# Batch 0's x turned by VectorE, the queries' weights loaded once, and three loads moved, in a cross-attention kernel on one core

## The chip, the cores and the metric

The kernel runs on one core of a Trainium2 chip. The time is the device time of one execution in microseconds (us), the median of several runs. A core has five engines, each with an instruction queue of its own: TensorE (PE in the profile; its weight loads are listed as PEld), VectorE (DVE), ScalarE (ACT), GpSimd (POOL) and SyncE (SP). SP does no arithmetic here; its queue issues most of the transfers (DMAs). ScalarE's queue issues a few too. Each issue holds its queue for about half a microsecond to one microsecond, and the data lands later.

## The reference

Attention of 8 batches of 112 queries over 375 context rows, of which the last 4 are "prompts" with a softmax of their own. There are 20 heads of 16 channels (320 channels); a context row has 512 elements. Everything is float32.

```python
text, ip = ehs[:, :-4], ehs[:, -4:]
q, k, v = heads(x @ W_q), heads(text @ W_k), heads(text @ W_v)
p = softmax(q @ k.T * 16 ** -0.5)
text_out = p @ v
k_ip, v_ip = heads(ip @ W_k_ip), heads(ip @ W_v_ip)
qsem = l2norm(p @ text)                  # 512 elements for each query and head
sem = qsem @ l2norm(ip).T
p_ip = softmax(q @ k_ip.T * 16 ** -0.5 + 0.5 * sem) * spatial_mask
out = (text_out + p_ip @ v_ip) @ W_out + b_out + x
```

## The kernel before

The work goes in steps (b, g): batch b, group g of four heads, five groups to a batch. A step n has the number 5b + g. In each step

- `multiplied` (L787 on) multiplies the transposed probabilities xgT by a table u, which holds the Gram matrix of the batch's context in blocks of 32 rows beside its values. The four results go to four banks ps_qd. From them come the length of qsem, its products with the prompts and the text's output, without qsem itself ever being formed;
- `scores` (L719) makes the scores of the step two ahead (`LEAD`), four of them, in the two banks ps_sc or, for one pair, the two banks ps_mm;
- `probabilities` (L754) takes the maximum nmx on VectorE (L751) and the exponential p on ScalarE (L765; for batches from 1 on with a copy ipl of the prompts' logits, L767). `sent` (L769, the issue at L772) sends p from SP to xg, which regroups queries by 32 rows, one transfer for a head;
- `turned` (L774) turns xg with VectorE's 32x32 transposes into xgT (L781) for the step after;
- `reduced` (L846) multiplies ps_qd by p and sums, on VectorE. With that, and with ScalarE's copy pvs (L813), the banks ps_qd are free for the next step.

Between the steps the engines make the next batch's tables: `values` (L611), `keys` (L577; its third block, heads 16 to 19, only transposes keys that `values` made on the side, L568), `gram` (L535), `project_queries` (L381). Batch 0 has its queries alone; batches 1 and 2, 3 and 4, and so on share a pass. For batch 0 x comes as rows, and TensorE turns it (L359, copied by ScalarE at L362); for the others x is loaded by `load_x_blocks` (four transfers, 28 rows by 4 by 80 elements, into xr_sb, which has two places), and VectorE turns it in 32x32 blocks (L369). The rows of the weights W_q must be in the matching order: `load_channels` gives the one for TensorE's way, `load_pairs` the one for VectorE's. So the queries' weights are loaded twice, at L133/L134 and again at L121/L122. `spread` (L143, L144) spaces the last four heads to 32 columns on GpSimd and is run after each.

The order of instructions on TensorE, VectorE and SP is the order in which the program is written. In the prologue, up to the first step, this holds for all engines. An engine takes its instructions in that order, and a wait at one holds up all behind it. In the prologue SP issues, in order: context of batch 0, the values' weights, x of batch 0, the queries' weights, the keys' weights, context of batch 1, twelve copies of ug into u (`gram_to_groups`, L553; four more go through ScalarE's queue), vr (values regrouped, L636, out of a copy vd that ScalarE sends at L627), xg of step 0, then the queries' weights again, x of batch 1, xg of step 1, the prompts' weights wkip and wvip (L137), and xg of step 2. At the end of step 0 follow the context of batch 2 (L160, L165) and x of batch 2 (`x_loads`, L127). `kip` (L328) holds the prompts' keys, `ps_ip` (L708) the prompts' logits of batch 0.

PSUM has eight banks in three rings: four ps_qd, two ps_sc, two ps_mm. `bank(name, spare)` (L85) takes the next of ps_mm, or with `spare` the next of ps_sc. A ring's next bank is free when the last reader of what was in it is done.

Of the kernel before, what the change touches and what calls it, by code (L numbers as in the profile page):

```python
# [8 lines left out]
F32 = mybir.dt.float32  # L9
# [11 lines left out]
def kernel(  # L21
# [14 lines left out]
    nc = tc.nc  # L36
    P = 128
    B, S, C = x.shape
# [46 lines left out]
    def bank(name, spare=False):  # L85

        if spare:
            return ps_sc.tile([P, 512], F32, tag="sc", name=name)
        return ps_mm.tile([P, 512], F32, tag="mm", name=name)
# [28 lines left out]
    def load_pairs(eng, t, w):  # L118

        w = w.rearrange("(p c) f -> p c f", c=5)  # L120
        eng.dma_start(t[0::2, :, :C], w[:, :3, :])  # L121
        eng.dma_start(t[1::2, :2, :C], w[:, 3:, :])  # L122

    def load_x_blocks(b, j):

        for a in range(QN):
            nc.sync.dma_start(  # L127
                xr_sb[a * RG : a * RG + S // QN, j, :, :XB],
                x[b, :, a * XB : (a + 1) * XB].rearrange("(q i) f -> i q f", q=QN),
            )  # L130

    def load_channels(eng, t, w):
        eng.dma_start(t[:, :FULL, :C], w[: FULL * P, :].rearrange("(i p) f -> p i f", p=P))  # L133
        eng.dma_start(t[:REST, FULL, :C], w[FULL * P :, :])  # L134

    def load_embed(eng, t, w):
        eng.dma_start(t[:, :, :C], w.rearrange("(p e) f -> p e f", e=NE))  # L137
# [48 lines left out]

    wv_in = work.tile([P, BLK, P], F32, tag="xgT", name="wv_in")
    wv_in = wv_in.rearrange("p j k -> p (j k)")[:, : NE * C].rearrange("p (e f) -> p e f", f=C)
    load_embed(nc.sync, wv_in, w_v)
    nc.sync.dma_start(x_sb[:, 0, :], x[0])  # L190
    load_channels(nc.sync, wq_sb, w_q)
    load_embed(nc.sync, wk_sb, w_k)
    loaded[1] = load_ctx(1)


    ident = const.tile([P, P], F32, tag="ident", name="ident")
    make_identity(nc, ident)
    nc.gpsimd.memset(wq_sb[REST:, FULL, :], 0.0)

    half = const.tile([P, NT, P], F32, tag="half", name="half")  # L200
    nc.gpsimd.memset(half, 1.0)
# [143 lines left out]
    def project_queries(bs):  # L345
        n = len(bs)
        end = bs[0] == B - 1
        xT = work.tile([P, NC, 2, QN, RG], F32, tag="xT", name=f"xT_{bs[0]}", bufs=1)
        qm = work.tile([P, NC, 2, 2 * S], F32, tag="qm", name=f"qm_{bs[0]}", bufs=2)

        qT = const.tile([P, NC, S], F32, tag="qT", name="qT") if bs[0] == 0 else None
        for j, b in enumerate(bs):
            queries[b] = (qT, qm, j)
        if qT is not None:
            nc.gpsimd.memset(xT[REST:, FULL, 0], 0.0)
            for i in range(NC):
                cn = min(P, C - i * P)
                ps = ps_qd.tile([P, 512], F32, tag="qd", name=f"ps_x_0_{i}")
                nc.tensor.transpose(  # L359
                    ps[:cn, :S], x_sb[:, 0, i * P : i * P + cn], ident[:S, :S]  # L360
                )
                nc.scalar.copy(  # L362
                    xT[:cn, i, 0, :, : S // QN],
                    ps[:cn, :S].rearrange("p (q i) -> p q i", q=QN),
                )
                yield
        for j in range(n if qT is None else 0):
            for e in range(NC):
                nc.vector.transpose(  # L369
                    xT[:, e, j],  # L370
                    xr_sb[:, j, :, e : e + XB]
                    .rearrange("p q (m c) -> p q m c", c=5)[:, :, :, 0:4:3],
                )
            yield
        for i in range(NC):
            if end and i == FULL:
                ps = ps_qd.tile([P, 512], F32, tag="qd", name=f"ps_q_{bs[0]}_{i}")
            else:
                ps = bank(f"ps_q_{bs[0]}_{i}")
            for j in range(NC):  # L380
                nc.tensor.matmul(  # L381
                    ps[:, : n * S],
                    wq_sb[:, j, i * P : (i + 1) * P],
                    xT[:, j, :n, :, : S // QN],
                    start=(j == 0),
                    stop=(j == NC - 1),
                )

            for r in range(2 if i < FULL else 1):
                nc.vector.tensor_scalar_mul(  # L390
                    qm[:, i, r, : n * S], ps[:, : n * S], emask[:, r : r + 1]
                )
            if qT is not None:
                nc.scalar.copy(qT[:, i, :], ps[:, :S])
            yield
# [162 lines left out]
    def keys(b):  # L558
        s = st[b]
        if b > 0:  # L560
            nc.gpsimd.tensor_copy(s["kT"][:, :, TT:], kip[:, :, b * NIP : (b + 1) * NIP])
        for i in range(NC):
            ps = bank(f"ps_k_{b}_{i}", spare=1 < b < B - 1 and i == FULL)
            if 0 < b < B - 1 and i == FULL:

                for c in range(NT):
                    rows = min(P, TT - c * P)
                    nc.tensor.transpose(  # L568
                        ps[:, c * P : c * P + rows],
                        s["k3"][:rows, c].rearrange("p a r d -> p (a r d)"),  # L570
                        ident[:rows, :rows],
                    )
                nc.scalar.copy(s["kT"][:, i, :TT], ps[:, :TT])
                yield
                return
            for e in range(NE):
                nc.tensor.matmul(  # L577
                    ps[:, :TT],
                    wk_sb[:, e, i * P : (i + 1) * P],
                    s["ctxT"][:, e, :TT],  # L580
                    start=(e == 0),
                    stop=(e == NE - 1),
                )
            nc.scalar.copy(s["kT"][:, i, :TT], ps[:, :TT])
            yield
# [545 lines left out]
    def run(key, make, pieces=1):  # L1131

        if key not in gens:
            gens[key] = make()
        for _ in range(pieces):
            next(gens[key], None)
# [63 lines left out]
    nc.scalar.preload_act_table(AF.Exp)  # L1200
    gram_to_groups(0, range(QN - 1))
    run(("v", 0), lambda: values(0))
    run(("q", 0), lambda: project_queries(pairs[0]), 3)
    gram_to_groups(0, (QN - 1,), nc.scalar)
    run(("v", 0), None, 2)
    values_to_dram(0, nc.scalar)
# [1 line left out]
    spread(nc.gpsimd, wq_sb)  # L1208
    nc.gpsimd.tensor_copy(wv_sb[:, :, C:], wk_sb[:, :, FULL * P : C])
    spread(nc.gpsimd, wk_sb)  # L1210
    nc.gpsimd.memset(xr_sb, 0.0)
    for xt in x_ring:
        nc.gpsimd.memset(xt, 0.0)
    run(("q", 0), None)
# [4 lines left out]
        probabilities(0, 0, a)  # L1219
    drain(transposed_context(1))  # L1220
    run(("q", 0), None)
    nc.gpsimd.memset(wq_sb[:, FULL, :], 0.0)
    load_pairs(nc.sync, wq_sb, w_q)
    load_x_blocks(1, 0)
    run(("k", 0), None)
    for a in range(GROUP):
        scores(0, 1, a, early=True)
        probabilities(0, 1, a)
    load_embed(nc.sync, wkip_sb, w_k_ip)
    load_embed(nc.sync, wvip_sb, w_v_ip)  # L1230
    placed(0, 0)
    drain(turned(0, 0, BLK))
    run(("k", 0), None)
    run(("v", 1), lambda: values(1))
    more_constants()
    spread(nc.gpsimd, wq_sb)
    prologue.close()

    def load_x(b0, b1):
# [2 lines left out]
    def load_rest(n):  # L1242
# [8 lines left out]


    x_loads = {
        (0, 0): ((0, 0), (2, 1)),
        (1, 0): ((3, 0), (4, 1)),
        (2, NG - 1): ((5, 0), (6, 1)),
        (4, NG - 1): ((7, 0),),
# [17 lines left out]
    for n, (b, g) in enumerate(steps[:-NG]):  # L1275
# [11 lines left out]
        for j, _ in enumerate(multiplied(b, g)):  # L1287
            if j == 0:
                for c, a in now if late else ():
                    scores(*c, a)  # L1290
                    probabilities(*c, a)
                if g == 3:
                    regrouped(b + 1, nc.gpsimd.tensor_copy, [(a, a) for a in range(GROUP)])
                    regrouped(b + 1, nc.scalar.copy, across[0])
                elif g == NG - 1:
                    regrouped(b + 1, nc.scalar.copy, across[2])
                for c, a in more:
                    scores(*c, a, ps=bank(f"ps_s_{c[0]}_{c[1]}_{a}"))
                    probabilities(*c, a, hold=True)
                if n == NG - 1:  # L1300
                    run(("c", LEAD), None)
            if j == 5:
                for c, a in then:
                    scores(*c, a)
                held = more + [(c, a) for c, a in then if c == steps[n + LEAD + 1]]
                for c, a in then:
                    probabilities(*c, a, hold=(c, a) in held)
                drain(turn)
                for c, a in held:
                    sent(*c, a)  # L1310
            if j == 2:
                if g == 0:
                    gram_banks(b + 1)
                turn = turned(*steps[n + 1], 2 * QN)
                next(turn)
                if 1 <= g <= 3:
                    gram_to_groups(b + 1, {1: (0,), 2: (1,), 3: (3,)}[g], parts=halves[g == 2])
                for c, i in x_loads.get((b, g), ())[: int(n > 0)]:
                    load_x_blocks(c, i)

                if g in (1, 2) and b > 0:
                    run(("f", b - 1), None)
# [43 lines left out]
    b = B - 1  # L1366
# [136 lines left out]
```

## Time and profile before

| | |
|---|---|
| median of 3 runs | 418.91 us (417.69 to 419.31) |
| the profiled execution's own time | 419.28 us |
| its span in the trace | 417.6 us |
| mean granted clock of TensorE | 0.999 |
| busy: TensorE, VectorE, ScalarE, GpSimd | 98%, 80%, 52%, 30% |
| steps 0, 1, 2, 3 start at | 37.06, 49.47, 58.83, 68.89 us |
| steps 4, 5, 6 start at | 79.32, 87.59, 97.95 us |

A row of the timeline gives the start, the busy time, the engine, the line and the operation with its output and inputs (`out<-in`), the tile as partitions by elements, and a count (xN) where rows were joined; the start is then that of the first and the time that of all. In brackets stands how long the engine was idle before it, and what released it. `SPq` and `ACTq` are the queues that issue transfers: their times are the times of issuing, not of the transfer. A row of the chain gives start, time and piece. The rows on which the argument rests are shown in the prediction.

### The profile page before, as it was taken

What the parts mean: (1) busy time and instruction counts of PE and PEld (TensorE: products, weight loads), DVE (VectorE), ACT (ScalarE), POOL (GpSimd) and SP (SyncE); (2) the same over time, 40 slices, a digit from 0 to 9 for tenths busy, and PEclk for the clock granted to TensorE, in tenths of its full rate; (3) what the DMA queues carried; (4) which work ended last, traced back from release to release, by engine and by line L of the source; (5) the groups of instructions that cost most, each with busy time, mean ns of one, the idle gap of its engine ahead of it and who ended that gap; (6) DMA issues with size and microseconds to landing.
All of it is one profiled execution on the core that took longest, in us unless ns stands there. A gap on an engine that the chain in (4) does not pass through costs nothing.

```text
span 417.6 us, 14139 instructions
## 1 busy us (share of the span) xinstructions
PE 410.9 (98%) x5505; PEld 322.8 (77%) x5505; DVE 333.9 (80%) x726; ACT 217.0 (52%) x730; POOL 123.3 (30%) x308
## 2 busy tenths in 40 slices
PE   8999999999999999999999999999999999999995
PEld 8866777878777877788778887788777987787893
DVE  4036688998798988899799988889888977889774
ACT  2344332746356363654538463553637553688773
POOL 3621121112052120712135120611207121555540
PEclk9999999999999999999999999999999999999999
DMA  8677946565954555545554455545544356444300
GB/s 252 187 192 198 187 111 163 143 169 132 195 152 118 151 149 146 140 125 153 143 142 127 127 154 142 145 106 153 163 119 115 92 167 162 130 129 127 111 2 31
DMA packets 47578, 58.98 MB, mean 141 GB/s; under 512 B 10648, under 2 KB 41536, under 8 KB 47510
## 3 DMA queue, kind: packets, MB, share of 16 engines
q1 hardware_dynamic: 46878, 57.10, 51.9%
q8 instruction: 44, 0.72, 0.8%
q10 hardware_dynamic: 632, 0.96, 0.8%
q14 instruction: 24, 0.20, 0.2%
HBM read 16.79 MB, written 1.88 MB: 45 GB/s over the span
## 4 chain that ended last, share of the span: by engine, by line
PE 90%; DMA 3%; DVE 2%; ACT 2%; issue 1%; SPq 1%; POOL 0%; DVEq 0%; ACTq 0%; POOLq 0%
PE ps_qd L800 38%; PE ps_v L611 15%; PE ps_s L729 10%; PE ps_k L577 10%; PE ps_g L535 7%; DMA xg<-p 3%; PE ps_o L1017 3%; PE ps_q L381 2%; PE ps_g L491 1%; PE ps_w L472 1%; DVE nmx L751 1%; PE ps_k L593 1%; PE ps_c L455 1%; ACT p L765 0%; DVE xgT L781 0%
## 5 line engine op out<-in xcount | busy, mean ns | idle before, releaser
L800 PE MATMUL ps_qd<-u,xgT 32*112 32x168 f32 (+11 forms) x3840 | 218.6, 350 | 0.0
L800 PEld LDWEIGHTS ps_qd<-u,xgT 32*112 32x112 f32 x3840 | 186.0, 172 | 26.1 <-DVE ss L846 1.3
L765 ACT ACTIVATE p<-ps_s,nmx 112x371 f32<-112x371 f32 x156 | 84.5, 579 | 91.2 <-DVE nmx L751 83.9
L781 DVE STREAM_TRANSPOSE xgT<-xg 128x512 f32<-128x512 f32 (+2 forms) x79 | 126.0, 1603 | 6.2 <-DMA xg<-p 4.6
L751 DVE TENSOR_REDUCE nmx<-ps_s 112x1 f32<-112x371 f32 x160 | 78.5, 535 | 26.2 <-PE ps_s L729 25.3
L846 DVE CUSTOM_DVE_ANT_0 junk<-ps_qd,p 112x371 f32<-112x371 f32 x146 | 79.3, 543 | 19.7 <-ACT pvs L813 4.0
L698 POOL COPY u<-vr 128x64 f32<-128x64 f32 x120 | 26.5, 239 | 137.3 <-PE ps_qd L800 104.9
L729 PE MATMUL ps_s<-kT,qm 32*112 32x375 f32 (+1 forms) x320 | 66.4, 496 | 0.0
L611 PE MATMUL ps_v<-wv_sb,ctxT 128*128 128x384 f32 (+1 forms) x192 | 63.0, 477 | 0.0
L611 PEld LDWEIGHTS ps_v<-wv_sb,ctxT 128*128 128x128 f32 x192 | 35.7, 190 | 20.9
L577 PE MATMUL ps_k<-ctxT,wk_sb 128*128 128x371 f32 x136 | 46.9, 488 | 0.2 <-DVE ctxT L463 0.2
L729 PEld LDWEIGHTS ps_s<-kT,qm 32*112 32x112 f32 x320 | 25.9, 171 | 12.3 <-issue 10.0
L577 PEld LDWEIGHTS ps_k<-ctxT,wk_sb 128*128 128x128 f32 x136 | 24.4, 189 | 14.1 <-issue 0.5
L646 ACT COPY vr<-vext 32x240 f32<-32x240 f32 x84 | 32.7, 389 | 1.2
L618 ACT COPY vext<-ps_v 128x384 f32<-128x384 f32 (+1 forms) x24 | 11.2, 466 | 41.0 <-PE ps_v L611 41.0
L535 PE MATMUL ps_g<-ctxT 128*32 128x375 f32 (+11 forms) x672 | 30.4, 333 | 0.0
L535 PEld LDWEIGHTS ps_g<-ctxT 128*32 128x32 f32 x672 | 27.7, 110 | 2.0
L767 ACT COPY ipl<-ps_s 112x4 f32<-112x4 f32 x140 | 23.1, 165 | 0.0
L992 POOL TENSOR_TENSOR wv<-vip,w 112x1280 f32<-112x1280 f32 x6 | 14.8, 2466 | 26.4 <-DVE w L929 26.4
L390 DVE TENSOR_SCALAR qm<-ps_q,emask 128x224 f32<-128x224 f32 (+1 forms) x25 | 9.0, 394 | 16.5 <-PE ps_q L381 16.5
L507 ACT ACTIVATE ug<-ps_g 128x375 f32<-128x375 f32 (+2 forms) x24 | 8.3, 375 | 24.6 <-PE ps_g L535 12.4
L442 DVE STREAM_TRANSPOSE ctxT<-ct 128x512 f32<-128x512 f32 x18 | 20.0, 1110 | 0.0
(174 smaller groups left out, 342.2 us busy)
## 6 DMA issues: line engine op xcount, KB each, us to landing
xg<-p SPq DMA_DIRECT2D x156, 162.3 KB
u<-ug SPq DMA_DIRECT2D x124, 99.0 KB
ct<-in_ctx_dram SPq DMA_DIRECT2D x24, 176.0 KB
vip<-vipd SPq DMA_DIRECT2D x6, 560.0 KB
out_dram<-ob SPq DMA_DIRECT2D x8, 140.0 KB
ct<-in_ctx_dram SPq DMA_DIRECT2D x4, 256.0 KB
x_sb<-in_x_dram SPq DMA_DIRECT2D x7, 140.0 KB
xr_sb<-in_x_dram SPq DMA_DIRECT2D x28, 35.0 KB
```

Source lines behind the costliest of these rows:

```text
L535: nc.tensor.matmul(ps[c][q * RG : (q + 1) * RG, j * RG - c * P : T - c * P], ctxT[:, e, j * RG : (j + 1) * RG], ctxT[:, e, j * RG : T], st ...
L577: nc.tensor.matmul(ps[:, :TT], wk_sb[:, e, i * P : (i + 1) * P], s["ctxT"][:, e, :TT], start=(e == 0), stop=(e == NE - 1),)
L611: nc.tensor.matmul(ps[:, :w], ctxT[:, e, c * P : (c + 1) * P], wv_sb[:, e, :w], start=(e == 0), stop=(e == NE - 1),)
L646: copy(s["vr"][a * RG : (a + 1) * RG, q::QN].rearrange("p c g d -> p c (g d)"), s["vext"][q * RG : (q + 1) * RG, :, a * w : (a + 1) * w],)
L698: nc.gpsimd.tensor_copy(v, dealt(b, c, s["vr"][:, c * QN : (c + 1) * QN, g, :]))
L729: nc.tensor.matmul(ps[:S, :w], qm[a * RG : (a + 1) * RG, i, r, j * S : (j + 1) * S], s["kT"][a * RG : (a + 1) * RG, i, :w], start=True, st ...
L751: nc.vector.tensor_reduce(nmx, s["sc", g, a][:S, :TT], AX.X, ALU.max, negate=True)
L765: nc.scalar.activation(s["p", g][:, a, :], ps[:S, :TT], AF.Exp, bias=nmx)
L767: nc.scalar.copy(s["ipl"][:, groups[g][a], :], ps[:S, TT:T])
L781: nc.vector.transpose(xT[:, j0:j1].rearrange("p j (k q) -> p q j k", q=QN), xg[:, :, j0 * RG : j1 * RG].rearrange("p q (j k) -> p q j k", ...
L800: nc.tensor.matmul(banks[a][:S, j * RG : UW], xT[a * RG : (a + 1) * RG, j, :S], region(b, c)[a * RG : (a + 1) * RG, q, j * RG - c * P :], ...
L846: nc.vector.tensor_tensor_reduce(out=junk, in0=ps[:S, :TT], in1=s["p", g][:, a, :], scale=1.0, scalar=0.0, op0=ALU.mult, op1=ALU.add, accu ...
```

## The change

- Batch 0's x is loaded by `load_x_blocks` into the second place of xr_sb, and VectorE turns it. TensorE's three transposes, ScalarE's three copies and a clearing of xT on GpSimd go. xr_sb is cleared first thing, since its loads now come early.
- The queries' weights are loaded once, by `load_pairs`, and spread once. Their third block is cleared ahead of that.
- x of batch 1 is loaded right behind the context of batch 1, ahead of the copies of u. x of batch 2 is loaded behind xg of step 0, where the second load of the weights and x of batch 1 stood, and wkip next to it, ahead of xg of step 1. wvip stays behind xg of step 1. At the end of step 0 no x is loaded any more.
- The third block of batch 1's keys takes a bank of ps_sc in place of one of ps_mm, as it does for later batches already.

```diff
+    ident = const.tile([P, P], F32, tag="ident", name="ident")
+    make_identity(nc, ident)
+    nc.gpsimd.memset(xr_sb, 0.0)
+    nc.gpsimd.memset(wq_sb[:, FULL, :], 0.0)
     load_embed(nc.sync, wv_in, w_v)
-    nc.sync.dma_start(x_sb[:, 0, :], x[0])
-    load_channels(nc.sync, wq_sb, w_q)
+    load_x_blocks(0, 1)
+    load_pairs(nc.sync, wq_sb, w_q)
     load_embed(nc.sync, wk_sb, w_k)
     loaded[1] = load_ctx(1)
-    ident = const.tile([P, P], F32, tag="ident", name="ident")
-    make_identity(nc, ident)
-    nc.gpsimd.memset(wq_sb[REST:, FULL, :], 0.0)
+    load_x_blocks(1, 0)
...
-        if qT is not None:
-            nc.gpsimd.memset(xT[REST:, FULL, 0], 0.0)
-            for i in range(NC):
-                cn = min(P, C - i * P)
-                ps = ps_qd.tile([P, 512], F32, tag="qd", name=f"ps_x_0_{i}")
-                nc.tensor.transpose(
-                    ps[:cn, :S], x_sb[:, 0, i * P : i * P + cn], ident[:S, :S]
-                )
-                nc.scalar.copy(
-                    xT[:cn, i, 0, :, : S // QN],
-                    ps[:cn, :S].rearrange("p (q i) -> p q i", q=QN),
-                )
-                yield
-        for j in range(n if qT is None else 0):
+        for j in range(n):
             for e in range(NC):
                 nc.vector.transpose(
                     xT[:, e, j],
-                    xr_sb[:, j, :, e : e + XB]
+                    xr_sb[:, j if qT is None else 1, :, e : e + XB]
...
-            ps = bank(f"ps_k_{b}_{i}", spare=1 < b < B - 1 and i == FULL)
+            ps = bank(f"ps_k_{b}_{i}", spare=0 < b < B - 1 and i == FULL)
...
-    run(("q", 0), lambda: project_queries(pairs[0]), 3)
+    run(("q", 0), lambda: project_queries(pairs[0]))
...
-    nc.gpsimd.memset(xr_sb, 0.0)
...
-    nc.gpsimd.memset(wq_sb[:, FULL, :], 0.0)
-    load_pairs(nc.sync, wq_sb, w_q)
-    load_x_blocks(1, 0)
+    load_x_blocks(2, 1)
+    load_embed(nc.sync, wkip_sb, w_k_ip)
...
-    load_embed(nc.sync, wkip_sb, w_k_ip)
     load_embed(nc.sync, wvip_sb, w_v_ip)
...
-    spread(nc.gpsimd, wq_sb)
...
-        (0, 0): ((0, 0), (2, 1)),
...
-                for c, i in x_loads.get((b, g), ())[: int(n > 0)]:
+                for c, i in x_loads.get((b, g), ())[:1]:
```

## The prediction

> **What bounds the kernel now.** I began with the page: busy shares, then the chain that ended last.
>
> ```profile
> span 417.6 us, 14139 instructions
> PE 410.9 (98%) x5505; PEld 322.8 (77%) x5505; DVE 333.9 (80%) x726; ACT 217.0 (52%) x730; POOL 123.3 (30%) x308
> PE 90%; DMA 3%; DVE 2%; ACT 2%; issue 1%; SPq 1%; POOL 0%; DVEq 0%; ACTq 0%; POOLq 0%
> ```
>
> TensorE is busy for 98% of the span and makes 90% of the chain. An edit can only pay in two ways: TensorE work taken out, or a place where TensorE waits. A wait shows little as idle time, because a stalled matmul counts as busy, so I compared whole steps in the timeline. A step is four heads: its scores (L729) open it, the score-by-context products (L800) fill it, and the next stage's first row ends it.
>
> ```profile
> 37.06 0.57 PE L729 MATMUL ps_s<-kT,qm 32*112 32x371 f32 x2
> 42.42 4.34 PE L535 MATMUL ps_g<-ctxT 128*32 128x375 f32 x96
> ...
> 58.83 0.57 PE L729 MATMUL ps_s<-kT,qm 32*112 32x371 f32 x2
> 64.70 2.76 PE L577 MATMUL ps_k<-ctxT,wk_sb 128*128 128x371 f32 x8
> ...
> 68.89 1.99 PE L800 MATMUL ps_qd<-u,xgT 32*112 32x392 f32 x8
> 75.50 2.76 PE L577 MATMUL ps_k<-ctxT,wk_sb 128*128 128x371 f32 x8
> ...
> 87.59 0.57 PE L729 MATMUL ps_s<-kT,qm 32*112 32x375 f32 x2
> 93.68 4.34 PE L535 MATMUL ps_g<-ctxT 128*32 128x375 f32 x96
> ```
>
> From start to start the first step takes 42.42-37.06 = 5.36 us. Step 2 takes 5.87 (some 0.2 of it three extra transposes of the prompts, so about 0.3 stalled), step 3 takes 6.61 (1.25 stalled), and step 5 takes 6.09 (0.73 stalled). The rest of the wait is in the same stretch. What the late steps wait for:
>
> ```profile
> 61.43 1.03 ACT L765 ACTIVATE p<-ps_s,nmx 112x371 f32<-112x371 f32 x2 [1.48 <-DVE nmx L751]
> 63.62 2.05 DVE L781 STREAM_TRANSPOSE xgT<-xg 128x1024 f32<-128x1024 f32 x1 [1.77 <-DMA xg<-p]
> 67.56 1.05 PEld L381 LDWEIGHTS ps_q<-xT,wq_sb 128*128 128x128 f32 x6 [0.69 <-ACT kip L328]
> 69.97 0.27 PEld L800 LDWEIGHTS ps_qd<-u,xgT 32*112 32x112 f32 x2 [0.43 <-DVE ss L846]
> 82.60 2.05 DVE L781 STREAM_TRANSPOSE xgT<-xg 128x1024 f32<-128x1024 f32 x1 [0.32 <-DMA xg<-p]
> 88.27 0.27 PEld L800 LDWEIGHTS ps_qd<-u,xgT 32*112 32x112 f32 x2 [0.40 <-DVE ss L846]
> 88.96 2.58 PEld L800 LDWEIGHTS ps_qd<-u,xgT 32*112 32x112 f32 x40 [0.43 <-DVE ss L846]
> ```
>
> Step 3 waits for VectorE's reductions (L846), which free the banks of the step before. VectorE was late because it sat 1.77 us waiting for the regrouped probabilities xg of step 3. Those go through SP's queue, so I read that next.
>
> ```profile
> 53.24 2.53 SPq L127 DMA_DIRECT2D xr_sb<-in_x_dram  x4
> 55.39 1.03 ACT L765 ACTIVATE p<-ps_s,nmx 112x371 f32<-112x371 f32 x2 [3.39 <-DVE nmx L751]
> 56.30 1.76 SPq L772 DMA_DIRECT2D xg<-p  x2
> 59.49 1.84 SPq L772 DMA_DIRECT2D xg<-p  x2
> ```
>
> The first pair of xg could go when its exponentials were there (about 52), but stood behind the load of x at 53.24. The second pair, ready at 56.42, stood behind that and went at 59.49 to 61.33, some 2.3 us before VectorE could start on it.
>
> **The change part by part.** *Batch 0's x.* The three TensorE transposes and ScalarE's copies go; three VectorE transposes come.
>
> ```profile
> 16.41 0.29 PE ps_x L359 x3
> 21.71 0.57 DVE L390 TENSOR_SCALAR qm<-ps_q,emask 128x112 f32<-128x112 f32 x2 [11.32 <-PE ps_q L381]
> 46.76 0.74 DVE L369 STREAM_TRANSPOSE xT<-xr_sb 128x128 f32<-128x128 f32 x3
> ```
>
> TensorE is the chain there: -0.29 us. The new transposes cost 0.74 us by the row of the same three for batch 1, and lie in 11.32 us in which VectorE has nothing to do; without that cover they would cost 0.74. Four loads of x (1.9 to 2.5 us of SP by such rows) replace one early on; the first reader comes only after 10 us, SP has issued its loads by then: 0.
>
> The Trainium skill, VectorE: DVE Perf Modes, section Rules for kernel authors, says to turn 128x128 on TensorE where a PSUM destination will do. That speaks against this part: by it the swap would be a loss of up to 0.74-0.29 = +0.45 us. The rows above disagree as long as VectorE is idle there.
>
> *The queries' weights, loaded once.* Out go two loads of 0.69 and 0.65 us (rows below) and a second spreading on GpSimd, which is 30% busy: 0 by themselves, but 1.34 us of SP's time and the bytes are free for what follows. Clearing wq and xr sooner on GpSimd is about 1 us there, and what it delays (the table `half`) is read only at 13 us: 0.
>
> *The loads' new order up to step 0.* Here a loss comes in. Batch 1's x now goes ahead of the copies of u.
>
> ```profile
> 15.08 8.15 SPq L553 DMA_DIRECT2D u<-ug  x12
> 16.80 0.59 ACTq L553 DMA_DIRECT2D u<-ug  x1
> 21.51 0.40 ACTq L627 DMA_DIRECT2D vd<-vext  x1
> 24.89 1.88 SPq L636 DMA_DIRECT2D vr<-vd  x4
> 27.00 3.71 SPq L772 DMA_DIRECT2D xg<-p  x4
> 30.81 0.69 SPq L121 DMA_DIRECT2D wq_sb<-in_L_xattn_W_q_dram  x1
> 31.55 0.65 SPq L122 DMA_DIRECT2D wq_sb<-in_L_xattn_W_q_dram  x1
> 32.26 1.88 SPq L127 DMA_DIRECT2D xr_sb<-in_x_dram  x4
> 33.70 2.97 DVE L781 STREAM_TRANSPOSE xgT<-xg 128x1536 f32<-128x1536 f32 x1
> 34.23 3.67 SPq L772 DMA_DIRECT2D xg<-p  x4
> 40.45 2.04 DVE L781 STREAM_TRANSPOSE xgT<-xg 128x1024 f32<-128x1024 f32 x1 [1.48 <-DMA xg<-p]
> SPq L165 <- DMA xg<-p: 4.2, 4, 2.2
> ```
>
> The last row (the table of waits: total, times, longest) shows loads of the context waiting for transfers of xg that they have nothing to do with. In the built program SP's and ScalarE's transfers share eight completion counters in rotation, and an issue waits until the transfer eight places ahead has landed. In the changed program SP's second copy of u stands eight places behind ScalarE's first, which cannot go before ScalarE's copy at 16.44. Before, twelve copies ran without a gap at 8.15/12 = 0.68 us each. ScalarE's first issue can end near 17.1; a landing of 1.6 us behind it (an estimate: the row of vd at 21.51 to its reader at 24.89 gives 3.4, the last xg issue at 37.90 to VectorE at 40.45 gives 2.55) puts SP's second copy at 18.7 instead of 15.76. Nine copies at 0.65 end at 24.6, two more at 25.9, vr takes 1.88, so xg of step 0 starts at 27.9 instead of 27.00. Its transpose began at 33.70, right behind the last landing, and ended at 36.67; 0.6 to 0.9 later it ends at 37.3 to 37.6, against 37.06-0.29 = 36.77 for TensorE. I take +0.5 us. Bounds: 0 (if the copies land sooner, or ScalarE's removed copies of x free it) and +1.6 (by the longer landings of the nearest rows, xg 1.8 late).
>
> The Trainium skill, DMA: Bandwidth & Descriptors, section Rules for kernel authors, has it that a load issued early and waited for late overlaps with the work between. By it the earlier load of batch 1's x costs nothing, the term is 0 and the sum rival A's -2.24. The row of 2.2 us speaks against it here: an early load can hold up a later issue that doesn't need it.
>
> After this SP catches up: the weights' loads (1.34 us) are gone, batch 1's x is in already, and batch 2's x takes its place. The prompts' weights stay inside the saturated stretch, one ahead of xg of step 1, one behind. That xg goes at about 34.2 as before.
>
> *Batch 2's x out of step 0's end.* The 2.53 us at 53.24 vanish. xg of step 3 can issue its first pair at about 52; its second pair follows the exponentials at 55 to 56.4 and ends near 57 to 58 instead of 61.33. Landing like before, 2.3 us later, gives about 59 to 60, against VectorE's need at 63.62-1.77 = 61.85. So the wait of 1.77 goes, VectorE runs up to 1.77 earlier, and the 1.25 of step 3 go too: -1.25 (bounds 0 and -1.25). Step 2 waits for a chain of the same VectorE work (exponentials at 61.43 wait 1.48 for nmx); with VectorE's earlier wait shortened I take all its 0.3: -0.3 (bounds 0, -0.3). TensorE's keys that start at 64.70 last 2.76, to 67.46, and the queries' products behind them start at 67.56, held by ScalarE's copy of kip, which stands behind the late exponentials: -0.1 (bounds 0, -0.1). Step 5: VectorE's wait of 0.32 at 82.60 goes, so -0.3 of its 0.73 (bounds 0, -0.73). What is late next is VectorE itself, still with ctxT and reductions in a row.
>
> *Another bank for the third key block of batch 1.*
>
> ```profile
> 84.69 0.54 PE L568 MATMUL ps_k<-ident,k 128*128 128x128 f32 x3
> 85.48 0.15 ACT L767 COPY ipl<-ps_s 112x4 f32<-112x4 f32 x1
> 86.89 0.76 PE L708 MATMUL ps_ip<-kipb,qT 128*112 128x32 f32 x6 [0.52 <-ACT kT L573]
> ```
>
> It frees ps_ip of waiting 0.52 us for kT's copy. But the score bank that the block now takes is in use until ScalarE has read the scores and ipl, at 85.63, and TensorE is there at 84.69: a new wait of up to 0.94, behind which the queries' products, ps_ip and the scores of step 5 stand. Both lie ahead of the same reductions, which set step 5's products anyway (0.40 and 0.43 of wait at 88.27 and 88.96). I take 0; bounds -0.52 and +0.45 (0.94 less 0.52, rounded up).
>
> **Sum:** -0.29 + 0.5 - 0.3 - 1.25 - 0.1 - 0.3 = -1.74 us. The profiled execution took 419.28 us (span 417.6 and 1.7 around it), which gives 417.5; it lies 0.37 above the median of 418.91, so the median should be about 417.2. (The other cases below are put against the median in the same way.)
>
> **The rivals.** *A, more is won:* step 0 loses nothing, as ScalarE's first copy lands sooner, and VectorE's lead reaches step 5. For it: only one counter stands between; against it: VectorE is 80% busy. -0.29-0.3-1.25-0.1-0.3 = -2.24 to -2.67 with all of step 5: 416.2 to 416.7.
>
> *B, the queue is late for good:* SP does not catch up after the copies of u, so that the second pair of step 3's xg still lands after 62. From there the stalls of steps 2, 3 and 5 all stay, and step 0's loss and the bank come on top: -0.29+1.6+0.45 = +1.76, and one more wait for a counter, at its longest 2.2, makes +3.96: 420.7 to 422.9; with step 0 at +0.5 and the bank at nothing only +0.2. For it: SP is full from 27 to 60, and the table shows 4.2 us of such waits. Against it: 1.34+2.53 = 3.87 us leave this queue.
>
> *C, hidden anyway:* step 3's banks come late for VectorE's own load, not xg. Then only -0.29 and +0.5 are left, +0.2: 419.1. Against it: VectorE sits idle for those 1.77 us.
>
> **How the numbers follow.** My sum 0.50, A 0.28, B 0.14, C 0.08. The sum's own range is 416.6 to 418. The range of 8 in 10 takes in A and the scatter of the runs (417.69 to 419.31), C and B's near end: 415.8 to 420.0. 0.5%, what a measurement of this kernel tells from none, is 2.1 us: faster by more, A and 0.08 of the sum's better end, 0.36; slower by more, 0.10 of B; the rest 0.54.
>
> **What would show it.** Right: no L359 on TensorE; SP's second copy of u some 3 us behind its first; step 0's transpose of xg ending after 37; no wait of 1.77 on VectorE near 62; step 3 near 5.4 us long; step 5 near 5.8. Wrong: step 3 still over 6 us, a gap of over 1 us ahead of step 0, or a wait at the third key block that moves the start of step 5.

## The result and the profile after

| | before | changed |
|---|---|---|
| median, 15 runs each | 417.78 us (416.36 to 419.31) | 420.93 us (418.69 to 421.97) |
| ratio, 95% interval | | 1.0071 [1.0052, 1.0090] |
| profiled execution, own time | 419.28 us | 421.48 us |
| its span | 417.6 us | 419.1 us |

The changed kernel is 3.0 us slower by the ratio (3.15 by the two medians); the forecast was 1.7 us faster. In the parts shown, a line of the changed kernel is 12 lower than in the one before (L729 is L717, L781 is L769, L772 is L760); in e6, e7, e10 and e11 it is 13 lower. The timeline of TensorE, by which the steps were measured before:

```profile
36.97 0.88 PE L717 MATMUL ps_s<-kT,qm 32*112 32x371 f32 x4
43.28 4.34 PE L523 MATMUL ps_g<-ctxT 128*32 128x375 f32 x96
49.81 2.85 PE L599 MATMUL ps_v<-wv_sb,ctxT 128*128 128x384 f32 x8 [2.19 <-ACT ug L495]
...
61.94 0.57 PE L717 MATMUL ps_s<-kT,qm 32*112 32x371 f32 x2
67.47 2.76 PE L565 MATMUL ps_k<-ctxT,wk_sb 128*128 128x371 f32 x8
...
71.30 1.28 PE L788 MATMUL ps_qd<-u,xgT 32*112 32x392 f32 x10
77.08 2.76 PE L565 MATMUL ps_k<-ctxT,wk_sb 128*128 128x371 f32 x8
...
80.90 0.57 PE L717 MATMUL ps_s<-kT,qm 32*112 32x375 f32 x2
86.81 0.54 PE L556 MATMUL ps_k<-ident,k 128*128 128x128 f32 x3 [0.48 <-ACT ipl L755]
88.94 0.57 PE L717 MATMUL ps_s<-kT,qm 32*112 32x375 f32 x2
94.82 4.34 PE L523 MATMUL ps_g<-ctxT 128*32 128x375 f32 x96
```

Read from start to start: step 0 takes 6.31 us (5.36 before). The Gram stage behind it takes 49.81-43.28 = 6.53 us (46.69-42.42 = 4.27 before): TensorE stands there for 2.19 us, where it did not stand before. The row of before that ends that stage:

```profile
46.69 2.85 PE L611 MATMUL ps_v<-wv_sb,ctxT 128*128 128x384 f32 x8
```

Step 2 takes 5.53 (5.87), step 3 5.78 (6.61), step 4 5.91 (84.69-79.32 = 5.37), step 5 5.88 (6.09). So steps 2, 3 and 5, which were to get shorter, did, by 1.38 us together, and step 0 and the Gram stage behind it got longer by 3.21. What step 4 loses comes back ahead of step 5, as the experiment on the bank shows. The chain of waits through the new stall (start, time, piece):

```profile
37.58 7.76 DMA xg<-p
...
45.46 2.21 DVE xgT L769
47.67 0.34 DVE nmx L739
...
48.04 0.55 ACT p L753 x2
...
48.96 0.41 ACT pvs L801 x4
49.37 0.39 ACT ug L495
...
49.81 2.85 PE ps_v L599 x8
```

The last transfer of xg of step 1, issued at 37.58, landed 7.76 us later. Behind its transpose on VectorE stand the maxima of step 2's second pair, behind these ScalarE's exponentials, behind them the copies pvs and the copy of the Gram matrix out of its bank (ug), and the next values on TensorE wait for that bank. The issues ahead, and VectorE's waits:

```profile
15.29 11.02 SPq L541 DMA_DIRECT2D u<-ug  x12
16.72 2.52 ACTq L541 DMA_DIRECT2D u<-ug  x4
26.36 2.16 SPq L624 DMA_DIRECT2D vr<-vd  x4
28.63 3.72 SPq L760 DMA_DIRECT2D xg<-p  x4
32.45 1.84 SPq L127 DMA_DIRECT2D xr_sb<-in_x_dram  x4
34.34 0.38 SPq L137 DMA_DIRECT2D wkip_sb<-in_L_xattn_W_k_ip_dram  x1
34.83 3.55 SPq L760 DMA_DIRECT2D xg<-p  x4
34.87 2.97 DVE L769 STREAM_TRANSPOSE xgT<-xg 128x1536 f32<-128x1536 f32 x1 [1.19 <-DMA xg<-p]
45.46 2.21 DVE L769 STREAM_TRANSPOSE xgT<-xg 128x1024 f32<-128x1024 f32 x1 [6.59 <-DMA xg<-p]
```

And from its table of waits:

```profile
SPq L541 <- DMA u<-ug: 2.9, 1, 2.9
```

xg of step 1 was issued at 34.83 to 38.38, some 0.5 us behind the kernel before (34.23 to 37.90). It landed at 37.58+7.76 = 45.34 us, and VectorE began on it at 45.46 in place of 40.45. The one thing that is new right ahead of it in the queue is wkip.

### The profile page after: what moved, and what is told of

Its sections match the earlier page's. It is cut to its first block, busy times and chain, and to the rows that moved or that the text cites. A ratio compares the mean times of both kernels' runs of the same rounds, so it can differ in the third digit from the quotient of the medians.

```text
span 419.1 us, 14127 instructions
## 1 busy us (share of the span) xinstructions
PE 409.9 (98%) x5502; PEld 322.1 (77%) x5502; DVE 335.4 (80%) x729; ACT 216.1 (52%) x727; POOL 121.4 (29%) x302
## 3 DMA queue, kind: packets, MB, share of 16 engines
HBM read 16.38 MB, written 1.88 MB: 44 GB/s over the span
## 4 chain that ended last, share of the span: by engine, by line
PE 92%; DVE 3%; DMA 3%; ACT 1%; issue 0%; DVEq 0%; ACTq 0%
PE ps_qd L788 39%; PE ps_v L599 15%; PE ps_k L565 11%; PE ps_s L717 10%; PE ps_g L523 6%; PE ps_q L369 3%; PE ps_o L1005 3%; DMA xg<-p 2%; PE ps_g L479 1%; DVE xgT L769 1%; DVE nmx L739 1%; DMA ct<-in_ctx_dram 1%; PE ps_k L581 1%; PE ps_c L443 1%; PE ps_k L556 1%
## 5 line engine op out<-in xcount | busy, mean ns | idle before, releaser
L769 DVE STREAM_TRANSPOSE xgT<-xg 128x512 f32<-128x512 f32 (+2 forms) x79 | 126.0, 1603 | 9.5 <-DMA xg<-p 8.1
L717 PE MATMUL ps_s<-kT,qm 32*112 32x375 f32 (+1 forms) x320 | 65.7, 495 | 0.0
L717 PEld LDWEIGHTS ps_s<-kT,qm 32*112 32x112 f32 x320 | 25.9, 171 | 12.5 <-issue 10.5
L496 POOL TENSOR_TENSOR ug<-ug,half 128x128 f32<-128x128 f32 (+1 forms) x24 | 10.4, 447 | 33.3 <-ACT ug L495 33.3
```

What stands on the lines that cost most here:

```text
L717: nc.tensor.matmul(ps[:S, :w], qm[a * RG : (a + 1) * RG, i, r, j * S : (j + 1) * S], s["kT"][a * RG : (a + 1) * RG, i, :w], start=True, st ...
L769: nc.vector.transpose(xT[:, j0:j1].rearrange("p j (k q) -> p q j k", q=QN), xg[:, :, j0 * RG : j1 * RG].rearrange("p q (j k) -> p q j k", ...
```

## The experiments

**One load put back, and the same load moved alone.** Theory T: wkip's 640 KB, issued ahead of xg of step 1, hold it up. R: x of batch 2 and the late copies of u do.

```diff
 changed kernel -> e1
-    load_embed(nc.sync, wkip_sb, w_k_ip)
     run(("k", 0), None)
...
+    load_embed(nc.sync, wkip_sb, w_k_ip)
     load_embed(nc.sync, wvip_sb, w_v_ip)
```

> The changed kernel with one load moved: wkip goes behind xg of step 1 again, next to wvip. Theory T (wkip, 655 KB on the same DMA engines, holds up the xg of step 1 that is issued behind it; it landed at 45.3 us, 7.0 us after its last issue at 38.38): xg lands within 3.5 us of its last issue, VectorE's wait of 6.59 us at step 0 falls under 2.5, the Gram stage behind step 0 goes from 6.5 back to 4.3-4.6 us, and the time falls by 1.8 to 2.6 us against the changed kernel: 0.6 to 1.5 us under the kernel before. Rival R (x of batch 2 and the copies of u, which are late, hold up xg; wkip is only a bystander): the Gram stage stays over 5.8 us and the time within 0.5 us of the changed kernel.

```diff
 kernel before -> e2
     load_x_blocks(1, 0)
+    load_embed(nc.sync, wkip_sb, w_k_ip)
     run(("k", 0), None)
...
-    load_embed(nc.sync, wkip_sb, w_k_ip)
     load_embed(nc.sync, wvip_sb, w_v_ip)
```

> The kernel before with one load moved: wkip ahead of xg of step 1, nothing else of the change. T: xg of step 1 lands 3 to 5 us later than the 40.4 us of before, VectorE waits 4 to 6.5 us for it, the Gram stage behind step 0 takes 5.5 to 6.5 us in place of 4.27, and the time rises by 1.2 to 2.5 us. R: Gram stage under 4.6 us, time within 0.4 us of before.

e1: 418.81 us, ratio to before 1.0024 [1.0009, 1.0039], so 0.0047 or 2.0 us of the loss gone, as T said, though not to below before. Timeline of e1:

```profile
40.43 2.04 DVE L769 STREAM_TRANSPOSE xgT<-xg 128x1024 f32<-128x1024 f32 x1 [1.59 <-DMA xg<-p]
43.22 4.34 PE L523 MATMUL ps_g<-ctxT 128*32 128x375 f32 x96
47.49 2.85 PE L599 MATMUL ps_v<-wv_sb,ctxT 128*128 128x384 f32 x8
```

VectorE's 6.59 us are 1.59, and the Gram stage is back at 47.49-43.22 = 4.27. e2: 420.41 us, 1.0062 [1.0040, 1.0085], 2.6 us slower than before by this one move. Timeline of e2:

```profile
34.41 0.38 SPq L137 DMA_DIRECT2D wkip_sb<-in_L_xattn_W_k_ip_dram  x1
34.88 3.66 SPq L772 DMA_DIRECT2D xg<-p  x4
42.62 4.34 PE L535 MATMUL ps_g<-ctxT 128*32 128x375 f32 x96
44.21 2.17 DVE L781 STREAM_TRANSPOSE xgT<-xg 128x1024 f32<-128x1024 f32 x1 [5.04 <-DMA xg<-p]
48.48 2.85 PE L611 MATMUL ps_v<-wv_sb,ctxT 128*128 128x384 f32 x8 [1.52 <-ACT ug L507]
```

The issue itself holds SP for 0.38 us; the transfer behind it comes 3.8 us later than before (44.21 to 40.45), though xg went into the queue only some 0.65 us later (34.88 to 34.23). R falls: here neither x nor u had been moved. In this execution, with 419.67 us one of the faster ones of e2, the Gram stage is 48.48-42.62-4.27 = 1.59 us longer; the 2.6 us are by the medians. Which property of the load holds xg up, its place in this queue or its traffic beside xg, is not shown: no run issues it from another queue.

**Both prompts' weights ahead.** Is it the amount?

```diff
 kernel before -> e9
     load_x_blocks(1, 0)
+    load_embed(nc.sync, wkip_sb, w_k_ip)
+    load_embed(nc.sync, wvip_sb, w_v_ip)
```

(and the two loads gone from behind xg of step 1)

> The kernel before with both prompts' weights (twice 655 KB) ahead of xg of step 1, in place of the one that cost 2.6 us. T (bytes ahead in the DMA engines): xg of step 1 lands another 2 to 4 us later than with one, VectorE's wait at step 0 grows from 5.0 to 7.5-9 us, and the time to 4.5-6.5 us above the kernel before. If it is the issue or the order in SP's queue and not the bytes: about 0.6 us (one issue) more than with one.

422.49 us, 1.0109 [1.0083, 1.0135]: 4.6 us, some 2 more than with one. The time is the one that T named, but it did not come about in T's way:

```profile
44.29 2.14 DVE L781 STREAM_TRANSPOSE xgT<-xg 128x1024 f32<-128x1024 f32 x1 [5.94 <-DMA xg<-p]
48.57 4.11 PE L611 MATMUL ps_v<-wv_sb,ctxT 128*128 128x384 f32 x8 [2.42 <-ACT ug L507]
```

VectorE's wait for xg of step 1 only grew from 5.04 to 5.94. Counted from the first issue of xg, its transpose begins 44.29-34.52 = 9.77 us later, against 44.21-34.88 = 9.33 with one load: 0.44 more, where T expected 2 to 4. So the delay did not grow in proportion to the bytes ahead, and this run speaks against T in that form. Most of the rest came behind it: the values take 4.04 us from start to start in place of 2.78 in e2, step 1 takes 5.73 in place of 5.36, together 1.63 us. There TensorE's granted clock reads 0.50 from 50 to 53 us, behind the 2.42 us in which TensorE stood; at the same place it reads 1.00 in e2 and in the changed kernel. In executions that were not profiled only the mean clock is known: it is 0.994 or 0.995 in five of e9's six, in three of the changed kernel's fifteen, and in two each of e2's and e3's six, and in the kernel before, as far as it is listed, never under 0.996. That the stall costs a second time in those, through the clock, is likely but not shown.

**Both weights later.**

```diff
 changed kernel -> e5 (both gone from the prologue)
         if n == 0:
+            load_embed(nc.sync, wkip_sb, w_k_ip)
+            load_embed(nc.sync, wvip_sb, w_v_ip)
             load_next(2)
```

> The changed kernel with both prompts' weights moved behind xg of step 2, to the end of step 0, ahead of batch 2's context. T: nothing large stands ahead of xg of step 1 or 2 any more: xg of step 1 lands within 3 us of its issue, the Gram stage takes 4.3 us, and the time falls by 2.2 to 3.2 us against the changed kernel, as long as the weights are there at 57 us for their products; if they are late, a new wait at the products (L308) of up to 2 us. Step 0 stays 0.9 us too long, since the copies of u are as late as before. R: no better than the changed kernel by more than 0.5 us.

418.74 us, 1.0016 [1.0002, 1.0030]: 2.3 us better than the changed kernel, as expected, and no better than e1. No wait came at the prompts' products. Step 0 stayed longer than expected, with 7.21 us in this execution (5.36 plus some 0.9 was expected).

**The bank.**

```diff
 changed kernel -> e3
-            ps = bank(f"ps_k_{b}_{i}", spare=0 < b < B - 1 and i == FULL)
+            ps = bank(f"ps_k_{b}_{i}", spare=1 < b < B - 1 and i == FULL)
```

> The changed kernel with the third key block of batch 1 in a bank of ps_mm again. If the bank is worth what the two traces say (step 4 longer by 0.55, the stages from there to step 5 shorter by 0.77): step 4 back at 5.4 us, those stages back at 2.9 us, time 0 to 0.5 us above the changed kernel. If the bank is what makes the change slower: 1 us or more under the changed kernel.

420.50 us, 1.0077 [1.0050, 1.0104], the same as the changed kernel within the intervals. Step 4 is back at 85.17-79.81 = 5.36 us; from the start of step 4 to the end of step 5 it takes 93.74-79.81 = 13.93, with the new bank 94.82-80.90 = 13.92. The wait only moves. (The stretch between the two steps, expected back at 2.9 us, takes 87.62-85.17 = 2.45.) Step 5 alone takes 5.87 or 5.88 us in the four profiles with the new bank and 6.09 to 6.12 in the ten with the old one, so what it gained in the changed kernel is the bank's. The same edit on e6, below:

> The run with x in turn, with the third key block of batch 1 in a bank of ps_mm again: the bank tried where nothing else is late. Step 4 takes 5.36 us in place of 5.96, and from its end to the end of step 5 0.4 to 0.7 us more; time within 0.4 us of that run, 0.2 to 0.9 us below the kernel before. If the bank costs or saves something there: over 0.5 us of difference.

417.08 us, 0.9975 [0.9957, 0.9992], against 0.9989 [0.9976, 1.0002]: intervals that overlap, and again 13.95 us from step 4 to the end of step 5 in both profiles.

**The first two parts alone.** Batch 0's x turned by VectorE and the weights loaded once, all moved loads and the bank as before (the diff is that of the change without these).

> Only the first two parts of the change: batch 0's x turned by VectorE and the queries' weights loaded once; the x of batches 1 and 2, the prompts' weights and the bank as before. TensorE loses its 0.29 us of transposes; SP loses 1.34 us of issues behind xg of step 0, so xg of step 1 and 2 go sooner. Expected: 0.1 to 0.8 us below the kernel before. If the new loads and transposes at the start cost something themselves: equal or above it.

417.25 us, 0.9989 [0.9974, 1.0004]: -0.5 us, not quite clear of nothing. Step 0 takes 5.35, step 2 5.53, step 3 5.78: the stalls of steps 2 and 3 are not there, with batch 2's x still loaded at the end of step 0.

**Batch 1's x ahead of the copies of u, alone.**

```diff
 e7 -> e8
     loaded[1] = load_ctx(1)
+    load_x_blocks(1, 0)
...
     run(("q", 0), None)
-    load_x_blocks(1, 0)
```

> The first two parts of the change (as in the run with turn and weights only) and one load moved: batch 1's x ahead of the copies of u. If this one move makes step 0 late (SP's second copy waits for ScalarE's first to land, eight transfers ahead): SP's second copy issues 3 us after its first, xg of step 0 is issued some 1.5 us later, step 0 takes 6.0 to 6.6 us in place of 5.36, and the time is 0.6 to 1.4 us above the run without the move. If it is not this load: the copies run without a gap, step 0 stays at 5.4 us, no difference over 0.3 us.

418.70 us, 1.0019 [1.0001, 1.0037]: 0.0030 or 1.25 us over e7. First e7's timeline, then e8's:

```profile
14.15 8.98 SPq L540 DMA_DIRECT2D u<-ug  x12
25.76 3.71 SPq L759 DMA_DIRECT2D xg<-p  x4
32.46 2.96 DVE L768 STREAM_TRANSPOSE xgT<-xg 128x1536 f32<-128x1536 f32 x1
```

```profile
15.15 10.98 SPq L541 DMA_DIRECT2D u<-ug  x12
34.72 2.96 DVE L769 STREAM_TRANSPOSE xgT<-xg 128x1536 f32<-128x1536 f32 x1 [1.18 <-DMA xg<-p]
36.83 0.88 PE L717 MATMUL ps_s<-kT,qm 32*112 32x371 f32 x4
37.78 3.42 PE L788 MATMUL ps_qd<-u,xgT 32*112 32x392 f32 x48
43.12 4.34 PE L523 MATMUL ps_g<-ctxT 128*32 128x375 f32 x96
```

The twelve copies take 11 us with the load ahead and 9 without; e8's table of waits has the same 2.9 us of SP for a copy of u that the changed kernel has. xgT then comes late and step 0 takes 43.12-36.83 = 6.29 us.

**Batch 2's x out of the end of step 0, alone.**

```diff
 e7 -> e11
     load_x_blocks(1, 0)
+    load_x_blocks(2, 1)
...
-        (0, 0): ((0, 0), (2, 1)),
```

> The first two parts of the change and one load moved: batch 2's x from the end of step 0 to behind xg of step 0, with nothing else of the new order. This is the step to which the forecast gave -1.25 us in step 3 and -0.3 in step 2. If it held: 1.2 to 1.6 us below the run with turn and weights only. By the later profiles (steps 2 and 3 take 5.53 and 5.78 us in all kernels but two executions of the one before, with or without this move): steps 2 and 3 at 5.5 and 5.8 us again, time within 0.5 us of the run with turn and weights only, 0 to 1 us below the kernel before.

417.30 us, 0.9988 [0.9971, 1.0004]: as e7. Step 3 in e11's timeline:

```profile
68.26 1.28 PE L787 MATMUL ps_qd<-u,xgT 32*112 32x392 f32 x10
74.04 2.76 PE L564 MATMUL ps_k<-ctxT,wk_sb 128*128 128x371 f32 x8
```

It takes 5.78 us, as in e7; step 2 takes 5.72 (5.53 in e7). The move to which the forecast gave 1.55 us brings nothing that can be measured behind the first two parts. That is a limit of this test: e7's profile has no such stall left to remove, and the move alone was not run on the kernel before.

**The kernel before, profiled twice more.**

> The kernel before, unchanged, profiled a second time. Its first profiled execution took 419.28 us, near the top of what it does (416.4 to 419.4, median 417.7). Theory H (the stalls of steps 2 and 3, 0.3 and 1.25 us, on whose removal the forecast rested, belong to that slow execution): step 2 takes 5.6 us or less, step 3 6.0 or less in an execution near the median, and the waits of 1.61 and 1.77 us of VectorE for xg are shorter by more than half. Rival S (they are there in every execution): step 3 takes 6.4 to 6.7 us again.

> The same as the run before it, a third profile of the unchanged kernel: H expects step 3 at 6.0 us or less in at least one of the two, S at 6.4 to 6.7 in both.

Timeline of the first of these (417.44 us):

```profile
58.41 0.57 PE L729 MATMUL ps_s<-kT,qm 32*112 32x371 f32 x2
61.47 2.06 DVE L781 STREAM_TRANSPOSE xgT<-xg 128x1024 f32<-128x1024 f32 x1 [0.71 <-DMA xg<-p]
63.94 2.76 PE L577 MATMUL ps_k<-ctxT,wk_sb 128*128 128x371 f32 x8
67.77 1.28 PE L800 MATMUL ps_qd<-u,xgT 32*112 32x392 f32 x10
73.55 2.76 PE L577 MATMUL ps_k<-ctxT,wk_sb 128*128 128x371 f32 x8
```

and of the second (418.31 us):

```profile
63.05 2.03 DVE L781 STREAM_TRANSPOSE xgT<-xg 128x1024 f32<-128x1024 f32 x1 [2.21 <-DMA xg<-p]
68.31 2.01 PE L800 MATMUL ps_qd<-u,xgT 32*112 32x392 f32 x8
74.94 2.76 PE L577 MATMUL ps_k<-ctxT,wk_sb 128*128 128x371 f32 x8
```

In the first, VectorE waits 0.71 us for xg of step 3, step 2 takes 5.53 us and step 3 5.78: the stalls that the prediction read are not there, in the unchanged kernel. In the second VectorE waits 2.21 and step 3 takes 6.63. H holds in its weaker form (one of the two): the stall comes in some executions. The one that was first profiled had it, and a span of 417.6 us where two sets of 23 runs of the same kernel had 416.1 and 415.8 in the mean. Step 3 takes 6.6 us in two of the five profiles with the old prologue (these three, e2, e9) and 5.8 in all nine with the new one. So the weights' second load, which is gone there, may have a part in the stall, or it may be chance; these few profiles can't tell.

**x in turn, weights later.**

```diff
 changed kernel -> e6
     loaded[1] = load_ctx(1)
-    load_x_blocks(1, 0)
...
-    load_x_blocks(2, 1)
-    load_embed(nc.sync, wkip_sb, w_k_ip)
+    load_x_blocks(1, 0)
...
-    load_embed(nc.sync, wvip_sb, w_v_ip)
+    load_x_blocks(2, 1)
...
         if n == 0:
+            load_embed(nc.sync, wkip_sb, w_k_ip)
+            load_embed(nc.sync, wvip_sb, w_v_ip)
             load_next(2)
```

> The changed kernel with the prompts' weights behind xg of step 2 (as in the run with the weights later) and the x loads put back: batch 1's behind xg of step 0, batch 2's behind xg of step 1, nothing ahead of the copies of u. If SP's late copies of u (second one at 18.9 us, when ScalarE's first had landed) make step 0 long: SP's twelve copies run without a gap, step 0 takes 5.4 us, and the time is 0.8 to 2.0 us below the run with the weights later, 0.1 to 0.9 us below the kernel before. If step 0 is long for another reason (VectorE's order, the new transposes), step 0 stays over 6 us and the time within 0.4 us of that run.

416.89 us, 0.9989 [0.9976, 1.0002]: 0.0027 or 1.1 us below e5, as expected; step 0 takes 5.36. No transpose of xg waits for a transfer any more. With the old bank (e10) the ratio is the lowest of the kernels run, 0.25% below before with an interval below 1. It overlaps those of e6, e7 and e11, so which of these four is fastest is not shown.

## Why the prediction was wrong

| term | forecast, us | measured, us | by |
|---|---|---|---|
| TensorE's three transposes, weights loaded once | -0.3 | -0.5 | e7 to before |
| step 0 (copies of u late) | +0.5 | +1.25 | e8 to e7 |
| steps 2 and 3 (batch 2's x moved) | -1.65 | 0, behind the first two parts | e11 to e7 |
| step 5 | -0.3 | 0 (its 0.2 are the bank's) | all profiles, by bank |
| bank | 0 | 0 | e3, e10 |
| wkip ahead of xg of step 1 | 0 | +2.0 to +2.6 | e1, e2 |

The first, second and last of these add up to -0.5+1.25+2.0 = 2.75 to 3.35 us, against 3.0 measured. Each has an interval of 0.6 to 1 us to both sides, so the agreement is no finer than that. If the stalls of steps 2 and 3 go with the weights' second load, what that saves is in the first row.

*The step that failed* is the sentence on the prompts' weights: "one ahead of xg of step 1, one behind. That xg goes at about 34.2 as before." It did go nearly so (34.83). But the prediction followed the queue's issues there and left out how much later xg lands behind such a load: it put at nothing, without a reason, a term that e1 and e2 measure at 2.0 and 2.6 us. The rows to see it by were at hand, in the timeline of the kernel before, where both weights' loads stand ahead of xg of step 2:

```profile
39.76 5.38 SPq L772 DMA_DIRECT2D xg<-p  x4
52.98 2.03 DVE L781 STREAM_TRANSPOSE xgT<-xg 128x1024 f32<-128x1024 f32 x1 [1.61 <-DMA ct<-in_ctx_dram]
```

Its last issue ended at 39.76+5.38 = 45.14, and its transpose began 7.84 us later, after a wait. (The row names a transfer of the context, but the transpose reads xg alone; the row of the waits in the prediction, `SPq L165 <- DMA xg<-p: 4.2, 4, 2.2`, shows the context's issues waiting for these same transfers.) The xg of step 1, with no such load right ahead, was turned 2.55 us behind its last issue. VectorE had other work until 51.37 in the one case; in the other it wants xg at 40.45-1.48 = 38.97, 1.07 us behind the last issue. The Trainium skill, DMA: Bandwidth & Descriptors, section Queues, rings and completion order, says that each DMA engine works through one queue's descriptors in the order of issue; e1 and e2 agree with it, with 5.0 and 3.8 us for the transfers behind 640 KB. That a second 640 KB adds only 0.4 us (e9) it does not explain.

*Step 0* was right in its mechanism, and mis-sized. SP's second copy of u went at 18.90, when ScalarE's first had landed at 18.88 (18.7 was forecast), but a further wait came in the row (12 copies in 11.0 us, forecast some 10.8), the loads of vr took 2.16 instead of 1.88, and xg went at 28.63, not 27.9. The forecast +0.5 lay below the measured loss, its bound +1.6 above it.

*Steps 2 and 3.* The waits were read rightly in the one execution that was shown, and they were taken for the kernel's. The profiled execution lay 0.37 us above the median of three runs, which seemed little; against the 15 runs of the result it lay 1.5 above. From the start of step 2 to the end of step 3 the two first profiles do differ by (75.50-58.83)-(77.08-61.94) = 1.53 us, close to the forecast 1.65: the term fits that one execution, and not the kernel's median. The stall of 1.25 us also had a floor that was not seen: step 3 takes 5.78 us, 0.42 above a normal step, in e6 too, where no transpose of xg waits for a transfer.

*Step 5* was taken to gain from VectorE's wait of 0.32 us. The wait is gone, but step 5 is no shorter by it (6.09 us with it, 6.11 without it in e8, same bank). What is shorter where VectorE does not wait is the stretch ahead of step 5: 2.90 and 2.96 us in the two profiles with the wait, 2.45 to 2.49 in the eight others with the old bank, one of them of the unchanged kernel.

*The bank*: the two bounds were taken to cancel, and do. *The rivals*: B had the right sign and the right time (420.7 to 422.9, with 0.14), but not this mechanism: SP does catch up, and steps 2 and 3 do not stall. Rival A's claim that step 0 loses nothing fell, and with it what the prediction drew from the rule named beside the sum, that the earlier load costs nothing: batch 1's x, issued early, cost 1.25 us. C said that the move of batch 2's x brings nothing; e11 agrees in the time, but C's reason, VectorE's own load, is not shown by it.

## What to carry to other kernels

When a load is moved, price it twice: the time its issue holds the queue, and the time by which whatever was queued behind it lands later. For the second, look in the same trace for a transfer that already stands behind such a load, and compare its landing with one that doesn't. Before a forecast rests on a stall, look at where the profiled execution lies among the runs: near the top of their spread, the stall may be what put it there, and a second and third profile of the unchanged kernel can tell.

## What the runs showed of the hardware

That a transfer in the way costs so much more than its issue was not expected: 640 KB took 0.38 us to issue, and the four transfers of 162 KB each behind it landed 3.8 (e2) to 5.0 us (changed kernel to e1) later, while a second 640 KB ahead added 0.4 us to that (e9). A stall can also be followed by a slower TensorE: in e9 the granted clock was 0.50 from 50 to 53 us behind 2.42 us of standing, and in the changed kernel's profile it stayed at 1.00 behind 2.19 us. Not expected either was the scatter at the start: the first long Gram stage began at 8.59 to 9.82 us in the nine profiles with the new prologue and at 9.00 to 9.81 in the five with the old one; its cause stays open. So single profiles were compared here by the lengths of steps, not by when they end.
